# The first expert's first 384 rows multiplied in the tail of the attention, with the last 512 destinations routed behind them

## The chip, the cores and the metric

The kernel runs on one core of one Trainium2 chip. The metric is the device time of one execution in microseconds (us); the median of 7 executions is compared. A profile is one further execution under the hardware profiler. Its engines are PE (matrix products; PEld is its weight load), DVE (vector), ACT (activation functions), POOL (GpSimd) and SP (which only starts DMAs); each runs its own instructions strictly in order.

## The reference

The model has 3125 nodes of 256 features and 103125 directed edges, and four residual blocks:

```python
x = x + gat3(layernorm(x), src, dst)          # three graph-attention layers
x = x + moe_top2(layernorm(x))                # 16 experts, two per node
x = x + relu(n @ W + segment_sum((n @ M)[src], dst)),  n = layernorm(x)
x = x + moe_top1(layernorm(x))                # 8 experts, one per node
```

An attention layer gives each destination the softmax-weighted sum of its sources' rows. In the second block a node's logits are `n @ gate_w + gate_b`; its two largest, as a softmax over those two, weigh the outputs of two experts, each `(silu(n @ w1[e]) * (n @ w2[e])) @ w3[e]` with a hidden width of 512. The change lies where the first block ends and the second begins.

## The kernel before, in words

**The third attention layer** (L1371 to L1534, `i == 2`, called `last`). The 3125 destinations are cut into 13 groups (`GROUPS`, L1133): twelve of 256, which are two tiles of 128 partitions, and one of 53. For a group, the loop over `s` goes through 25 tiles of sources. DVE makes the weights `pm` of 128 sources by 256 destinations (L1448), and PE multiplies them into `acc` in PSUM (L1451), once for each of the two destination tiles; every such product is recorded as two PE instructions. Six `pm` buffers (pool `dp`) let DVE run ahead. The short group packs six source tiles into one `few` (L1439, L1441), and PE multiplies it at L1443. `acc` has two buffers, so that one group can be divided while the next is multiplied.

What follows a group is put in the list `later` (L1503 to L1506) with the step `s` of the next group at which it is written into the program: `divide` (L1476) at 8, `norm` at 9, `gate` at 11, `send` at 14, all some steps earlier for the group before the short one (`sooner`, L1502). The framework's scheduler then orders each engine's instructions, by priorities and its own model, and sets all waits; only inside `tc.manual_schedule()` (before: the second layer alone, L1403) does the order written by hand stand.

**The router** (`Router.group`, L608). `norm` takes mean and variance of each row (L619, L620), the square root on ACT (L621), loads ACT's table for the exponential ahead (`table`, L552 and L622), and writes the attention's output to `sums` in DRAM (L624), to which the experts' outputs are added later. `gate` normalises a row (L632), transposes it on PE (L637), copies it (L639), multiplies it by `gate_w` (L641) and adds the bias (L642). `send` finds the two largest logits with two runs of `first_max` (L241 to L249), makes the two weights (L650 to L656), counts the rank of each node among those sent to its expert by two small products (L664, L665) with a running sum `pre` (L662), turns it into a row number in `rows0` (L667 to L673), and sends the node's row, with its number and weight behind it, to that place for both experts by indirect DMAs of POOL (L680). `rows0` holds NP = 3200 rows for each expert; the expert takes the first 384 (`EACH` = 3 tiles), and what goes beyond is handled in "more" slots of 64 rows. `finish` (L686) makes the table of these slots, after 32 products (L693) of which nothing is read but which keep PE running.

**The experts** (`routed_experts`, L727). `turn(e)` loads 384 rows (L748) and transposes them (L753, L754); `fetch(e)` loads the expert's three weights of 512 KB; `first` multiplies by `w1` and `w2` (L778) with SiLU (L781) and product (L782); `second` multiplies by `w3` (L793), weighs (L796) and adds into `sums` by an indirect DMA of POOL that accumulates (L798). After the experts 3, 5, 7, 9 and 11 a pair of "more" slots runs (`first_more`, L805), with weights in `room`; if there are more than ten slots, the branch at L880 runs the others. At the end `sums` is read back (L886). All 16 experts go through this loop.

**Buffers.** The pool `big` has two large buffers. During the third layer one holds that layer's sources and the other the layer's output `y_out` (L1379); then `room` takes the sources' buffer.

## Time and profile before

| what | us |
| --- | --- |
| median of 7 runs (lowest, highest) | 1880.77 (1872.89, 1882.78) |
| the profiled execution, its own time | 1868.43 |
| its span, first to last instruction | 1866.7 |
| PE busy in the span | 1775.3 (95%) |
| DVE / ACT / POOL busy | 1016.2 / 722.1 / 491.3 |
| last product of the third layer ends (L1443) | at 1059.32 |
| first product of expert 0 starts (L778) | at 1083.07 |
| first product of expert 1 starts (L778) | at 1099.49 |

All places in time are microseconds from the start of the span. A row of the timeline gives start, duration, engine, line, operation, output and inputs with their shape, the number of instructions merged into the row (x4), and in brackets how long the engine stood idle before it and what ended that. A row of the table by stretches gives the stretch, its length, the busy time of each engine with its instructions, TensorE's granted clock as a share of full speed, the busy share of the DMA engines and GB/s. The chain of waits follows the work that ended last backwards, in order of time.

### The profile page before, as it was taken

The numbers are of one execution on the slowest core, as the hardware profiler recorded it, in microseconds if no ns is written. First come the engines' busy times: TensorE is split into PE (matmuls) and PEld (weight loads), VectorE is DVE, ScalarE is ACT, GpSimd is POOL, SyncE is SP. The second block draws the span as 40 slices with busy tenths as digits, with TensorE's granted clock in tenths as the row PEclk, the third lists the DMA queues.
The fourth block names the chain that finished last, engine by engine and source line by source line (L and its number), as shares of the span: only waits on it lengthen the run. The fifth ranks groups of instructions, "written<-read, shape, count | busy, mean of one in ns | idle before, by whom it ended". The sixth has DMA issues, their size and how long they took to land. (4 is left out here: it accounts for less than half of the span.)

```text
span 1866.7 us, 27222 instructions
## 1 busy us (share of the span) xinstructions
PE 1775.3 (95%) x9225; PEld 1383.8 (74%) x9225; DVE 1016.2 (54%) x2875; ACT 722.1 (39%) x2072; POOL 491.3 (26%) x634
## 2 busy tenths in 40 slices
PE   6999999999798999999999799999989999999997
PEld 4788888887577887788888666666668887455786
DVE  6888888875466777677777622222244222333221
ACT  3766767671011111122222211121127999455221
POOL 4210110000566775032322322333310000122121
PEclk9999999999899999999999899999999999999999
DMA  4111223757333332121111285877430000723894
GB/s 116 33 46 48 66 63 136 316 225 298 78 83 85 87 87 77 30 66 40 49 44 43 73 248 156 239 199 191 110 89 1 1 1 1 237 117 153 258 301 125
DMA packets 123698, 215.43 MB, mean 115 GB/s; under 512 B 14795, under 2 KB 86641, under 8 KB 123512
## 3 DMA queue, kind: packets, MB, share of 16 engines
q1 hardware_dynamic: 83700, 134.23, 21.5%
q0 software_dynamic: 24704, 56.84, 11.7%
q10 hardware_dynamic: 15138, 22.44, 3.8%
q8 instruction: 79, 1.29, 0.3%
q14 instruction: 77, 0.63, 0.1%
HBM read 122.54 MB, written 92.61 MB: 115 GB/s over the span
## 5 line engine op out<-in xcount | busy, mean ns | idle before, releaser
L1451 PE MATMUL acc<-big,pm 128*128 128x257 f32 x3400 | 796.8, 386 | 22.2 <-issue 15.6
L1451 PEld LDWEIGHTS acc<-big,pm 128*128 128x128 f32 x3400 | 633.4, 192 | 116.8 <-issue 20.1
L1448 DVE SCALAR_TENSOR_TENSOR pm<-tau,big,counts 128x256 f32<-128x256 f32 x850 | 398.6, 487 | 139.3 <-PE acc L1451 113.0
L1994 POOL DMA_INDIRECT apart_row<-apart_rows,apart_who x172 | 179.7, 1045 | 94.1 <-issue 44.2
L778 PE MATMUL ps_h<-xsT,w 128*128 128x384 f32 x512 | 168.4, 487 | 0.6 <-ACT xsT L754 0.6
L1603 PE MATMUL acc<-msg,cr 128*128 128x512 f32 (+1 forms) x625 | 157.9, 403 | 0.1
L778 PEld LDWEIGHTS ps_h<-xsT,w 128*128 128x128 f32 x512 | 96.8, 190 | 66.9 <-issue 1.9
L1603 PEld LDWEIGHTS acc<-msg,cr 128*128 128x128 f32 (+1 forms) x625 | 114.7, 185 | 29.2 <-ACT cr L1599 1.2
L1599 ACT ACTIVATE cr<-counts 128x256 fp32r<-128x256 uint8 (+1 forms) x325 | 130.5, 402 | 14.1 <-PE acc L1603 7.0
L1860 ACT CAST counts<-acc_c 128x500 uint8<-128x500 f32 (+1 forms) x155 | 96.0, 678 | 94.5 <-PE acc_c L1850 94.2
L1835 DVE TENSOR_TENSOR ohk<-iota_k,key 128x2016 f16<-128x2016 f16 (+1 forms) x79 | 94.4, 1195 | 20.4 <-PE acc_c L1850 20.2
L781 ACT ACTIVATE silu<-ps_h 128x384 f32<-128x384 f32 x64 | 31.4, 490 | 182.2 <-PE ps_h L778 180.1
L798 POOL DMA_INDIRECT sums<-y,who x48 | 74.7, 1556 | 92.7 <-DVE y L796 71.0
L782 DVE TENSOR_TENSOR hid<-silu,ps_h 128x384 f32<-128x384 f32 x64 | 35.4, 554 | 112.6 <-PE ps_h L778 107.7
L1829 ACT ACTIVATE ohs<-iota_s,low 128x128 f16<-128x128 f16 x286 | 94.1, 401 | 0.0
L936 PE MATMUL ps_H<-big,t_w 128*128 128x512 f32 (+1 forms) x224 | 93.1, 552 | 0.8 <-ACT H L938 0.5
L1351 ACT ACTIVATE yT<-ps_m 128x256 f32<-128x256 f32 (+1 forms) x25 | 9.5, 379 | 204.0 <-PE ps_m L1349 173.8
L1064 PE MATMUL ps_y<-t_wd,hsT 128*128 x384 | 87.1, 379 | 0.3 <-ACT hsT L1112 0.3
L793 PE MATMUL ps_o<-w,hid 128*128 128x256 f32 x384 | 87.2, 379 | 0.0
L1850 PEld LDWEIGHTS <-ohs 128*128 128x128 f16 x1250 | 77.7, 98 | 10.9
L1850 PE MATMUL acc_c<-ohk,ohs 128*128 128x125 f16 x1250 | 84.5, 218 | 0.0
L1221 PE MATMUL ps_m<-we,yT 128*128 128x258 f32 (+1 forms) x248 | 71.7, 409 | 11.5 <-ACT yT L1351 6.1
(398 smaller groups left out, 2159.6 us busy)
## 6 DMA issues: line engine op xcount, KB each, us to landing
rows<-empty SPq DMA_DIRECT2D x16, 2564.0 KB
w<-in_L_ffn_w_dram ACTq DMA_DIRECT2D x42, 512.0 KB
big<-in_L_ffn_w_dram SPq DMA_DIRECT2D x30, 512.0 KB
hs<-rows SPq DMA_DIRECT2D x23, 641.0 KB
rows<-empty SPq DMA_DIRECT2D x16, 516.0 KB
t_wd<-in_L_ffn_Wd_dram SPq DMA_DIRECT2D x8, 1024.0 KB
big<-in_L_ffn_Wd_dram SPq DMA_DIRECT2D x6, 1024.0 KB
xs<-rows SPq DMA_DIRECT2D x15, 387.0 KB
```

The source lines that it names most:

```text
L778: nc.tensor.matmul(ps, w[:, k, j * P:(j + 1) * P], xsT[:, k], start=(k == 0), stop=(k == KD - 1))
L793: nc.tensor.matmul(ps, hid[:, j, q * P:(q + 1) * P], o[:, j], start=(j == 0), stop=(j == nh - 1))
L936: nc.tensor.matmul(ps[:, :n], a[:, k, j * P:(j + 1) * P], xnT[:, k, c:c + n], start=(k == 0), stop=(k == KD - 1))
L1448: nc.vector.scalar_tensor_tensor(pm[:, :n], tau[:, :n], now.rho[:, of:of + 1], edges[:, of, :n], op0=OP.max, op1=OP.mult)
L1451: nc.tensor.matmul(acc[:r, j, :D + 1], pm[:, q:q + r], now.h[:, of, :D + 1], start=(s == 0), stop=(s == NT - 1))
L1599: nc.scalar.activation(cr[:, :n], edges[:, s, :n], AF.Copy, accum_out=seen[:, a * NT + s:a * NT + s + 1])
L1603: nc.tensor.matmul(acc[:r, j].rearrange("p h d -> p (h d)"), cr[:, q:q + r], msg[:, s].rearrange("p h d -> p (h d)"), start=(s == 0), stop ...
L1829: nc.scalar.activation(far[:, i], self.iota_s, AF.Abs, scale=-1.0, bias=self.low32[:, batch, i:i + 1])
L1835: nc.vector.tensor_tensor(to[:, i:tiles].rearrange("p t (x u) -> p t x u", u=2), iota.rearrange("p (x u) -> p x u", u=2)[:, None].to_broad ...
L1850: nc.tensor.matmul(acc[:, u], ohs[:, i], ohk[:, i, :KEYS], start=(t == 0), stop=(t == TW - 1))
L1860: nc.scalar.copy(to[:, :, d0 % PAIR:d0 % PAIR + whole * WIN].rearrange("p s (u d) -> p u s d", u=whole), acc[:, :whole])
L1994: nc.gpsimd.indirect_dma_start(out=row[:, j], out_offset=None, in_=self.table[:, :], in_offset=bass.IndirectOffsetOnAxis(ap=self.who[:, q ...
```

## The change: what it does

1. **Order of the third layer's parts** (`LAST_PARTS`): groups 0 to 9, then the short group, then group 10 (tiles 20, 21), then group 11 cut into two parts of one tile (22, 23). The group before the short one is divided beside it, but normalised, gated and sent one part later, beside group 10 (`more = NT`). Tile 23's routing comes after all attention products.
2. **Expert 0's rows are settled early.** After the short group is sent, `reserve` raises the first free place of expert 0 to 384 if fewer nodes have come so far, so that the last 512 destinations (tiles 20 to 23) lie behind its first 384 rows. `expert.load` then loads these rows on SP, behind the scatters of all tiles sent so far; `expert.turn` transposes them at step 16 of the last part. Expert 0's weights are loaded at the layer's start into the buffer that was `y_out`'s; `y_out` becomes a small tile for each part.
3. **The tail is written by hand** (`tc.manual_schedule()`): tile 23's routing stands first on each engine, and expert 0's products, SiLUs and second products lie between its steps. `first(acc, j, u)` is a quarter of `w1` (u = 0) or `w2` (u = 1): four PE instructions. `finish` comes in three pieces between them; its 32 idle products go.
4. **The expert loop starts at 1.** Expert 1's weights, rows and transposed rows lie in `room`, its weights are fetched by SP as soon as the layer's sources are free. Expert 0's outputs are scattered after that (`expert.send`), and expert 1's scatters wait for them. Experts 2 and 3 are fetched by SP behind expert 1's transposed rows.
5. The last block's hidden weights (`hidden_weights`) are asked for in the third part of the layer rather than after it.

The diff, cut to its core:

```diff
+def behind_all(tc, made, others):
+
+    for other in others:
+        tc.add_manual_dep(made.ins, other.name, mybir.DependencyInfo(mybir.DependencyClass.Sync, mybir.DependencyReason.DATA),
+                          reason="rows of different tokens")
+    return made
...
+    def reserve(self, pp):
+
+        nc = self.nc
+        ps = pp.tile([P, 1], F32, name="ps_z")
+        nc.tensor.matmul(ps, self.every, self.pre[:, self.sent, 0:1], start=True, stop=True)
+        nc.vector.tensor_scalar(self.bump, ps, -1.0, float(EACH * P), op0=OP.mult, op1=OP.add)
+        nc.vector.tensor_scalar(self.bump, self.bump, 0.0, None, op0=OP.max)
+        nc.vector.tensor_tensor(self.first[:, 0:1], self.first[:, 0:1], self.bump, op=OP.add)
...
+        def again(i, t):
+            other = rp.tile([P, ROW0], F32, name="row2")
+            nc.scalar.copy(other[:, :D], own[i][:, :D])
+            for row in (own[i], other):
+                nc.gpsimd.tensor_copy(row[:, D:D + 1], self.node[:, t:t + 1])
+            others.append(other)
...
-            table(nc, wp, rstd[:, 1], AF.Exp)
+            table(nc, wp, rstd[:, 1], AF.Silu if apart else AF.Exp)
...
+                if between:
+                    between()
...
-            if t0 + n == NT - 1:
+            if before_last:
                 table(nc, wp, m2, AF.Sqrt)
-            nc.vector.tensor_scalar(wt[:, 0], m2, 1.0, None, op0=OP.add)
-            nc.vector.reciprocal(wt[:, 0], wt[:, 0])
-            nc.vector.tensor_tensor(wt[:, 1], m2, wt[:, 0], op=OP.mult)
+
+            def weigh():
+                nc.vector.tensor_scalar(wt[:, 0], m2, 1.0, None, op0=OP.add)
+                nc.vector.reciprocal(wt[:, 0], wt[:, 0])
+                nc.vector.tensor_tensor(wt[:, 1], m2, wt[:, 0], op=OP.mult)
+            if not apart:
+                weigh()
             sel = wp.tile([P, n, NX0], BF16, name="g_sel")
...
+            if apart:
+                weigh()
...
+                if not apart:
+                    again(i, t)
+                for j, row in enumerate((own[i], others[i])):
...
-        nc.scalar.copy(self.pre[0:1, 0], total)
-        keep_warm(nc, pp.tile([P, (NT + 1) * NX0], F32, name="ps_x"), self.every, self.pre.rearrange("p t e -> p (t e)"), 32)
+        places = cp.tile([1, NX0], F32, name="more_total")
+        nc.vector.tensor_copy(places, total)
+        nc.vector.tensor_tensor(places[:, 0:1], places[:, 0:1], self.bump[0:1], op=OP.add)
+        total = places
+        yield
...
+        yield
...
+    def load(self, scatters):
+        behind_all(self.tc, self.nc.sync.dma_start(self.xs, self.rows[:EACH * P].rearrange("(q p) f -> p q f", p=P)),
+                   scatters)
+
+    def turn(self, pp):
+        nc = self.nc
+        for q in range(EACH):
+            ps = pp.tile([P, KD, P], F32, name="ps_m")
+            for k in range(KD):
+                nc.tensor.transpose(ps[:, k], self.xs[:, q, k * P:(k + 1) * P], self.ident)
+            nc.scalar.copy(self.xsT[:, :, q * P:(q + 1) * P], ps)
+        nc.gpsimd.tensor_copy(self.who, self.xs[:, :, D])
+
+    def first(self, ap_, j, u):
+        nc = self.nc
+        if u == 0:
+            self.ps[j] = ap_.tile([P, 2, CHUNK], F32, name="acc")
+        for k in range(KD):
+            nc.tensor.matmul(self.ps[j][:, u, :EACH * P], (self.a, self.b)[u][:, k, j * P:(j + 1) * P], self.xsT[:, k],
+                             start=(k == 0), stop=(k == KD - 1))
+
+    def glu(self, j):
+        nc, ps = self.nc, self.ps.pop(j)
+        nc.scalar.activation(self.hid[:, j], ps[:, 0, :EACH * P], AF.Silu)
+        nc.vector.tensor_tensor(self.hid[:, j], self.hid[:, j], ps[:, 1, :EACH * P], op=OP.mult)
+
+    def second(self, pp, q):
+        nc, nh = self.nc, HID0 // P
+        ps = pp.tile([P, D], F32, name="ps_m")
+        for j in range(nh):
+            nc.tensor.matmul(ps, self.hid[:, j, q * P:(q + 1) * P], self.o[:, j], start=(j == 0), stop=(j == nh - 1))
+        nc.vector.tensor_scalar(self.xs[:, q, :D], ps, self.xs[:, q, D + 1:D + 2], None, op0=OP.mult)
+
+    def send(self):
+        self.scatters = [
+            independent(self.tc, "sums0", self.nc.gpsimd.indirect_dma_start(
+                out=self.sums[:, :], out_offset=bass.IndirectOffsetOnAxis(ap=self.who[:, q:q + 1], axis=0),
+                in_=self.xs[:, q, :D], in_offset=None, bounds_check=NP + CAP0 - 1, oob_is_err=True, compute_op=OP.add))
+            for q in range(EACH)]
+
...
         def turn(e):
-            xs = xp.tile([P, nq, ROW0], F32, name="xs")
-            for q, n in ((0, nq),) if e else ((0, 1), (1, 1), (2, nq - 2)):
+            xs = xs_1 if e == 1 else xp.tile([P, nq, ROW0], F32, name="xs")
+            for q, n in ((0, nq),) if e > 1 else ((0, 1), (1, 1), (2, nq - 2)):
                 at = e * NP + q * P
-                nc.sync.dma_start(xs[:, q:q + n], rows[at:at + n * P].rearrange("(q p) f -> p q f", p=P))
-            xsT = xp.tile([P, KD, EACH * P], F32, name="xsT")
+                dma = nc.sync.dma_start(xs[:, q:q + n], rows[at:at + n * P].rearrange("(q p) f -> p q f", p=P))
+                if e == 1:
+                    behind_all(tc, dma, expert.rows_sent)
+            xsT = xsT_1 if e == 1 else xp.tile([P, KD, EACH * P], F32, name="xsT")
...
+            a, b, o = weights_1 if e == 1 else [pool.tile([P, k, f], F32, name=name) for pool, k, f, name in (
+                (ep, KD, HID0, "w1"), (ep, KD, HID0, "w2"), (op_, nh, D, "w3"))]
+            if 1 < e < 4:
 
                 for to in (a, b, o):
                     nc.gpsimd.tensor_copy(to[:, 0, 0:1], behind)
-            dma = (nc.sync if 0 < e < 3 else nc.scalar).dma_start
+            dma = (nc.sync if e < 4 else nc.scalar).dma_start
             dma(a, w1[e].rearrange("(k p) h -> p k h", p=P))
             dma(b, w2[e].rearrange("(k p) h -> p k h", p=P))
...
+                independent(tc, f"sums{e}", made)
+                if e == 1:
+                    behind_all(tc, made, expert.scatters)
...
-        turned = turn(0)
+        weights = fetch(1, None)
+        turned = turn(1)
+        expert.send()
+        x = block(big)
         behind = turned[1][:, 0, 0:1]
-        for e in range(NX0):
-            a, b, o = fetch(e, behind)
-            if e == 2:
+        for e in range(1, NX0):
+            a, b, o = weights if e == 1 else fetch(e, behind)
+            if e == 3:
                 load(behind)
             xs, xsT = turned
             hid, s = first(xsT, a, b)
...
+PARTS_OF = [(a, c, n) for a, (c, n) in enumerate(GROUPS)]
+LATE = 3
+LAST_PARTS = PARTS_OF[:10] + PARTS_OF[12:] + PARTS_OF[10:11] + [(11, 11 * PAIR + q, P) for q in (0, P)]
...
-                    y_out = block(big)
-                    nc.gpsimd.memset(y_out[:, NT - 1], 0.0)
+                    expert = make_first(block(big, ROW).rearrange("p t d -> p (t d)"))
...
-                for a, (c, n) in enumerate(GROUPS):
-                    if apart_now and a < APART:
-                        continue
+                parts = LAST_PARTS if last else PARTS_OF[APART:] if apart_now else PARTS_OF
+                for here, (a, c, n) in enumerate(parts):
                     tiles = [(q, (c + q) // P, min(P, n - q)) for q in range(0, n, P)]
+                    following = parts[here + 1:here + 2]
+                    short = bool(following) and following[0][2] <= P // 2
 
                     edges = counts_of(counts, a)
+                    if c > GROUPS[a][0]:
+                        edges = edges[:, :, c - GROUPS[a][0]:]
...
+                        if last and (a, s) == (2, 0):
+                            during(expert.a[:, 0, 0:1])
...
+                    if last:
+                        y_out = wl.tile([P, KD, D + 2], F32, name="we")[:, :, :D]
+                        if n <= P // 2:
+                            nc.gpsimd.memset(y_out[:, 0], 0.0)
...
-                    sooner = 2 if a == len(GROUPS) - 2 else 5 if i == 0 and a == len(GROUPS) - 1 else 0
-                    later.append((8 - sooner, divide))
-                    if last:
-                        norm, gate, send = router.group(wp, rp, zp, y_out, tiles[0][1], len(tiles))
-                        later += [(9 - sooner, norm), (11 - sooner, gate), (14 - sooner, send)]
+                    sooner = 2 if short else 5 if i == 0 and a == len(GROUPS) - 1 else 0
+                    if last and following:
+                        norm, gate, choose, send, again = router.group(wp, rp, zp, y_out, tiles[0][1], len(tiles),
+                                                                before_last=len(parts) - here == 2)
+                        more = NT if short else 0
+                        if len(parts) - here == 2:
+                            sooner = 4
+                        later += [(8 - sooner, divide), (9 - sooner + more, norm), (11 - sooner + more, gate),
+                                  (14 - sooner + more, choose), (14 - sooner + more, send)]
+                        if len(parts) - here == LATE + 1:
+                            later += [(14, lambda: router.reserve(zp)), (14, lambda: expert.load(router.scatters))]
+                        if len(parts) - here == 2:
+                            later.append((16, lambda: expert.turn(pp)))
+                    elif last:
+                        norm, gate, choose, send, again = router.group(wp, rp, zp, y_out, tiles[0][1], len(tiles), apart=True)
...
-            router.finish(wp, zp, over)
+            def between():
+                expert.first(ap_, 1, 0)
+                expert.glu(0)
+                again()
+                table(nc, wp, expert.hid[:, 0, 0:1], AF.Exp)
+
+            with tc.manual_schedule():
+                divide()
+                expert.first(ap_, 0, 0)
+                expert.first(ap_, 0, 1)
+                norm()
+                gate(between)
+                expert.first(ap_, 1, 1)
+                expert.first(ap_, 2, 0)
+                expert.first(ap_, 2, 1)
+                choose()
+                send()
+                finish = router.finish(wp, zp, over)
+                next(finish)
+                expert.glu(1)
+                expert.first(ap_, 3, 0)
+                expert.first(ap_, 3, 1)
+                expert.glu(2)
+                next(finish)
+                expert.glu(3)
+                for _ in finish:
+                    pass
+                for q in range(EACH):
+                    expert.second(pp, q)
...
+        def during(behind):
+            hidden.extend(hidden_weights(nc, early, *(i["L1_ffn_" + n] for n in ("W1", "b1", "Wg", "bg")), behind))
```

## The prediction

> **What bounds the kernel now.** I read the table of busy time by stretches first, then PE's timeline in the stretch that is not full, then the chain of waits. PE is busy for 95% of the span, so only a stretch where it lacks work can give time. By stretches, over the end of the third attention layer and the start of the experts:
>
> ```profile
> 1032.60:1052.20 19.60, 19.60 (x98) 16.63 (x96) 13.19 (x51) 4.96 (x10) 4.96 (x11) 1.00 0.04 14
> 1052.20:1059.40 7.20, 7.04 (x56) 3.56 (x55) 5.10 (x18) 2.80 (x7) 2.91 (x7) 1.00 0.26 91
> 1059.40:1083.10 23.70, 12.78 (x61) 7.06 (x61) 14.32 (x83) 5.82 (x15) 7.03 (x14) 0.71 0.36 113
> 1083.10:1099.50 16.40, 16.40 (x63) 11.49 (x64) 3.19 (x6) 4.40 (x8) 2.96 (x11) 1.00 1.00 342
> ```
>
> PE is full before 1059.40 and after 1083.10. Between them it counts 12.78 us, and PE's timeline shows what this is:
>
> ```profile
> 1060.60 0.62 PE L641 MATMUL ps_z<-gate_w,g_xT 128*128 128x16 f32 x4 [0.37 <-ACT g_xT L639]
> 1064.94 0.21 PE L664 MATMUL ps_z<-g_sel,before 128*128 128x32 bf16 x1 [3.73 <-DVE g_sel L660]
> 1065.14 0.19 PE L665 MATMUL ps_z<-pre,every 128*128 128x32 bf16 x1
> 1066.93 0.69 PE L637 MATMUL ps_x<-ident,row 128*128 128x128 f32 x2 [1.61 <-DVE row L632]
> 1068.08 1.04 PE L641 MATMUL ps_z<-gate_w,g_xT 128*128 128x16 f32 x4 [0.46 <-ACT g_xT L639]
> 1072.25 0.20 PE L664 MATMUL ps_z<-g_sel,before 128*128 128x16 bf16 x1 [3.13 <-DVE fm_hot L249]
> ...
> 1073.17 7.94 PE L561 MATMUL ps_x<-pre,every 128*128 128x416 bf16 x32 [0.25 <-ACT pre L692]
> 1081.64 0.85 PE L753 MATMUL ps_x<-ident,xs 128*128 128x128 f32 x6 [0.53 <-DMA xs<-rows]
> ```
>
> 7.94 of the 12.78 are products nobody reads; the rest serves the routing of the last tiles, which DVE, ACT, POOL and DMA carry. So some 24 us pass from the last attention product (1059.32) to expert 0 (1083.07), and then the chain is all PE:
>
> ```profile
> 1083.07 10.59 PE ps_h L778 x32
> 1093.65 0.66 PE ps_x L753 x6
> 1094.31 5.18 PE ps_o L793 x24
> 1099.49 5.80 PE ps_h L778 x18
> ```
>
> Expert 1 starts at 1099.49, that is 40.2 us after the last attention product. I call that product's end T0 and count from it; the change is worth what it takes from these 40.2 us, less what it adds ahead of T0.
>
> **From T0 to expert 1, routing.** One tile is routed after T0 instead of three. Divide: last time 1052.28 (end of products) to 1053.3 with one tile, mean and variance from T0+1.1. Row ready 1.6 later, by the single tile's rows: 0.46 (from 1062.57 to 1063.03), 0.20, the root 0.29 and the way to and from ACT, reciprocal 0.2, row 0.45: 2.7. Transposes 0.44: 3.15. The copy waits on ACT for the new SiLU table, loaded ahead behind the root (1.28 plus 0.20): 3.5, done 3.9. PE meanwhile makes 4 instructions of the expert (32 take 10.32, so 1.29): 4.45; gate 0.5: 4.95. From the bias at 1069.16 to the sum at 1072.40 DVE took 3.2: 8.15. The rank stands on PE behind 12 more expert instructions (3.87): 8.8, so 9.2. Rank to place numbers 1072.52 to 1073.56, and a hop: 10.3. From there to the second scatter's issue 1073.56 to 1076.55: 13.3. Landing: the rows were asked for at 1078.71, but the chain names DVE's last table entry (L724, ends 1078.52) for it, so 2.16 is an upper bound: 15.4. Rows asked for to first product 1078.71 to 1083.07, 4.36: expert 1 could start at **T0+19.8**.
>
> **From T0 to expert 1, expert 0's own work.** Last `first` quarters: `acc` has two buffers, so j = 3 waits for `glu(1)`, which DVE does after the place numbers: 10.3, two small operations 0.35, product 0.55: 11.2. Two quarters: 13.8. `second`: 3 x 1.73. Here a new wait is late: `ps_m` has two buffers, and the third `second` needs DVE's weighing of the first, which stands behind `glu(3)` (0.65) and the long piece of `finish` (1074.79 to 1078.52: 3.75): 18.2, weighed 18.7. The third product ends at 20.4, and expert 1's transposes and copy (1081.64 to 1083.07: 1.43) put its first product at **T0+21.8**. This is later than the routing, so I take it: 21.8 against 40.2 is **-18.4**. The idle products' 7.94 lay beside DVE, POOL and the DMA, and are worth nothing by themselves.
>
> **The clock.** Granted 0.71 in the stretch after 1059.40: after 3.73 us of idle PE, two transposes took 0.69 where 0.41 is usual. My sum leaves gaps of under 2 us. If one grew to that size, expert 1 would start slow: the idle products came back from 0.62 within some 4.4 us, so at most 2.2.
>
> A rule that speaks against the change: the tail needs the tables Sqrt, SiLU, Exp, SiLU. The trace has the load at 1.28, and the next activation 0.02 later:
>
> ```profile
> 1066.01 1.28 ACT L555 ACT_TABLE_LOAD   x1
> 1067.31 0.20 ACT L555 ACTIVATE table<-g_rstd 128x1 f32<-128x1 f32 x1
> ```
>
> The Trainium skill, "ScalarE: Activation LUTs", What ACT_TABLE_LOAD costs, gives the load about 1.28 us too, but adds a drain of 1.38 us to every switch. With two loads ahead of what PE waits for (before the copy, before `glu(1)`) that would be an estimate of 2.8 us off the gain. The rows above show no such drain, so the sum stands without it.
>
> **Ahead of T0.** The same attention products are made. Added on PE: in the old order 18 to 23 were routed before T0 but for the gate of 22 and 23; now 18 to 22 and 24 are. That is two single routings (0.38 + 0.51 + 0.4 each, from L637, L641, L664, L665) less 0.44: about +2.0. Expert 0's transposes, 0.85, and `reserve`, 0.2. Together +3.0, since PE is full there. The terms (L1337) stay the same in sum.
>
> DVE is the open point. A pair of tiles has a period of 23.8 us (L637 at 1014.43 and 1038.26) with DVE busy 17.8 in such a period, 25 x 0.48 of it for `pm`. A one-tile part halves PE's products (10.8) but not DVE's fixed cost. The trace has no `pm` of 128 x 128; neighbours are 0.48 (128 x 256) and 0.21 (`few`, 128 x 53). I take 0.30, between them by width. Part 22: 7.5 and the pair's routing 5.8 make 13.3 against PE's 12.9. Part 23: 7.5 and a single routing 5.2, 12.7 against 12.6. The part of group 10, with two routings beside it: 23.5 against 25. So DVE and PE are level, and six `pm` buffers now cover 6 x 0.43 instead of 6 x 0.87. I take 1.5 us of stalls. With 0.21 there are none; with 0.48 the two parts would lack some 9.
>
> T0 moves by 3.0 + 1.5 = **+4.5**.
>
> **Costs taken at nothing.** `expert.load` blocks SP until the scatters of 21 tiles have landed; the rows of `x` for tiles 22 and 23 and the `sums` stores queue behind it. Those scatters end some 3 us into part 22 (group 10's 25 us cover choice, places and six issues of 1.28), the rows come 5 us later, the transposes stand 13 us later still. Expert 0's 1.5 MB at the layer's start and the hidden weights (now asked for at 792.7, used at 1591) meet DMA at 0.12 to 0.14 busy. Expert 1's weights are asked for at T0 and have 21 us. Expert 1's scatters wait on POOL for expert 0's; an accumulation took 9.01 (1371.35), so about 2 us of waiting, with only other scatters and index casts behind. The first slots' 3 MB must wait until expert 1 has left `room` (T0+38) and are needed 28 us later; at 342 GB/s (1083.10 to 1099.50) they take 9.
>
> **Sum.** -18.4 + 4.5 = -13.9 from expert 1 on, where everything follows as before. The profiled execution took 1868.43, so 1854.5. It lies below all seven timed runs; against their median, 1880.77 - 13.9 = **1867**.
>
> **Rivals.**
> (a) *The gain is partly given back*, -7, 1874. Either DVE's `pm` is nearer 0.48 (+7), or expert 2's weights are late: SP takes them only behind POOL copies (L764), which may queue behind expert 0's three scatters (1.61 + 0.30 each, so 5 us after expert 1's start); 1.5 MB at 342 GB/s take 4.6, in time for 15.5; with the slots' 3 MB ahead of them, 5.5 late. For it: SP did issue a slot's load (1082.44) ahead of weights (1083.29). Against: the new slot loads can't start then.
> (b) *Slower: the routing chains lie open in the one-tile parts.* Place: parts 22 and 23. DVE waits in order for ACT's root and table, PE's gate and rank, with `pm` behind. One open chain is what now passes from 1059.36 to 1073.56, 14.2; six buffers cover 2.6; two open parts cost 23.2, giving -18.4 + 3.0 + 23.2 = +8, 1889. It decides from 15 us of stalls on. Against it: in the pair periods the same chain leaves PE 0.24 idle.
> (c) *It doesn't do what it says.* If more than ten slots were needed, L880's branch would run eleven pairs, each at least 9 us of loads: about +100, 1980. Counted from the reference's inputs, expert 0 gets 394 nodes outside the last 512, so `reserve` adds nothing, and the slots stay at exactly ten. Under 0.01.
> (d) *More*: T0+19.8 holds and DVE doesn't stall, -20.4 + 3.0 = -17.4, 1863.
>
> **How the numbers follow.** 0.2% is 3.8 us, about what a measurement of this kernel can tell from no change. Forecast and (d) 0.60, (a) 0.24, all faster: 0.84. Same 0.06 (stalls between (a) and (b)). Slower 0.10, nearly all (b). Range 1859 to 1877: (d) with a median that itself moves by some 4 (the seven lie within 10), up to where (a) ends.
>
> **What would show it.** Right: first products of L778 for expert 1 near 1086, PE full from T0 but for gaps of 1 to 2 us before j = 3 and the third `second`; no L561 at the tail; parts 22 and 23 of some 13 us each. Wrong: DVE without a gap in those parts and PE waiting for `pm`; the third `second` late for another reason than DVE's weighing of the first; PE idle inside expert 1 for weights.

## The result and the profile after

The changed kernel takes **1865.63 us** (median of 14 runs) against 1880.77 us (35 runs): a ratio of 0.9916 with the interval 0.9898 to 0.9934, so 12 to 19 us faster. The forecast was 1867, within 1859 to 1877.

The profiled execution took 1862.84 us (span 1861.0). That is only 5.6 less than the profiled execution before, and here a whole span misleads. The third layer's first product comes at 766.88 in the one and at 773.77 in the other, although the change touches little ahead of it. Over all profiled executions that point lies between 722 and 782 us, and the runs on one of the chips, where the kernel before takes 1827 us instead of 1880, have it at 722 to 736 throughout. So I compare stretches inside an execution, from points that every variant has: L3, the third layer's first product; T0, the last attention product's end; E1 and E2, the first products of expert 1 and expert 2, each by its own start in PE's timeline. For the kernel before that is 1099.33:

```profile
1099.33 10.48 PE L778 MATMUL ps_h<-xsT,w 128*128 128x384 f32 x32
```

The 1099.49 of the table of times before and of the prediction is the place of that product in the chain of waits, which gives it to PE only when the product before it has ended. So the prediction's 40.2 is 40.0 here, and 0.2 of the difference in the second row below is only this.

| us | before | after | change | forecast |
|---|---|---|---|---|
| L3 to T0 | 292.44 | 295.45 | +3.0 | +4.5 |
| T0 to E1 | 40.0 | 24.85 | -15.2 | -18.4 |
| E1 to the end | 767.38 | 766.97 | -0.4 | 0 |
| L3 to the end | 1099.83 | 1087.27 | -12.6 | -13.9 |

E2 to the end, which no edit touches, takes 749.4 to 752.8 us over all profiles, so -0.4 behind E1 can't be told from nothing.

These are the stretches of the profile after, with the columns of the first fence of the prediction: the busy time of PE, weight loads, DVE, ACT, POOL, each with its instructions, then the granted clock, the DMA share and GB/s.

```profile
1018.30:1043.60 25.30, 25.26 (x129) 21.72 (x129) 19.65 (x93) 7.83 (x17) 7.46 (x14) 1.00 0.10 33
1043.60:1056.60 13.00, 12.54 (x62) 9.91 (x61) 11.42 (x45) 3.41 (x8) 3.01 (x7) 1.00 0.24 70
1056.60:1069.00 12.40, 12.40 (x66) 10.33 (x65) 11.62 (x72) 6.76 (x13) 5.37 (x12) 1.00 0.15 53
1069.00:1094.10 25.10, 20.58 (x79) 13.30 (x78) 14.81 (x65) 7.92 (x15) 8.45 (x13) 0.93 0.48 147
```

The rows are the part of group 10, the two one-tile parts 22 and 23, and the tail from T0 (1069.22) to E1 (1094.07). The parts have the forecast lengths (25, about 13 and 13) and PE is full in them but for half a microsecond. Before, PE was busy for 12.78 of the 23.7 us up to expert 0's first product, 7.94 of them for products that nobody reads, and expert 0 then took 16.4 more; now it is busy for 20.58 of the 25.1 us up to expert 1's, and all of that is read by somebody. What PE does there, by its timeline of the profile after (the bracket is the idle time before the first instruction of a row, and who ended it):

```profile
1069.05 2.75 PE L811 MATMUL acc<-big 128*128 128x384 f32 x8
...
1073.83 4.13 PE L811 MATMUL acc<-big 128*128 128x384 f32 x12
1077.79 0.17 PE L706 MATMUL ps_z<-g_sel,before 128*128 128x16 bf16 x1
...
1080.10 4.42 PE L811 MATMUL acc<-big 128*128 128x384 f32 x8 [1.65 <-DVE big L817]
1084.32 3.81 PE L823 MATMUL ps_m<-big 128*128 128x256 f32 x16
1087.96 0.82 PE L867 MATMUL ps_x<-ident,big 128*128 128x128 f32 x6
1089.83 1.99 PE L823 MATMUL ps_m<-big 128*128 128x256 f32 x8 [1.05 <-DVE big L824]
...
1093.37 0.30 PE L867 MATMUL ps_x<-ident,xs 128*128 128x128 f32 x1 [1.43 <-DMA xs<-rows]
```

L811 is `first`, L823 `second`, L867 the transposes of a routed expert's rows (`big` holds expert 1's, `xs` expert 2's). Two of the three waits were foreseen, j = 3 for `glu(1)` and the third `second` for DVE. The third wait and one duration were not. Eight instructions of `first` take 2.75 at 1069.05 and **4.42** at 1080.10. And the wait of 1.43 is for the rows of **expert 2**, whose transposes stand ahead of expert 1's first product. The chain of waits of the profile after says why those rows are late:

```profile
1089.18 0.20 DVE more L771
1089.38 0.02 issue
1089.40 0.02 SPq L860
...
1089.51 3.30 DMA xs<-rows
1092.81 0.56 issue
1093.37 0.30 PE ps_x L867
```

SP asks for them (L860) only when DVE has written the last entry of the slot table (L771): the theory is that the rows' buffer lies where `finish` had its temporary tiles, and tables_apart below tests it.

### The profile page after: what moved, and what is told of

Its sections match the earlier page's. It is cut to its first block, busy times and chain, and to the rows that moved or that the text cites. A ratio compares the mean times of both kernels' runs of the same rounds, so it can differ in the third digit from the quotient of the medians.

```text
span 1861.0 us, 27219 instructions
## 1 busy us (share of the span) xinstructions
PE 1769.3 (95%) x9196; PEld 1380.6 (74%) x9196; DVE 1019.9 (55%) x2933; ACT 727.2 (39%) x2080; POOL 490.6 (26%) x634
## 5 line engine op out<-in xcount | busy, mean ns | idle before, releaser
L1577 PE MATMUL acc<-big,pm 128*128 128x257 f32 x3400 | 797.8, 386 | 20.3 <-issue 12.7
L1574 DVE SCALAR_TENSOR_TENSOR pm<-tau,big,counts 128x256 f32<-128x256 f32 (+1 forms) x875 | 401.5, 478 | 123.8 <-PE acc L1577 104.7
L891 PE MATMUL ps_h<-xsT,w 128*128 128x384 f32 x448 | 147.3, 487 | 0.0
L891 PEld LDWEIGHTS ps_h<-xsT,w 128*128 128x128 f32 x448 | 84.7, 190 | 58.0 <-issue 1.9
L911 POOL DMA_INDIRECT sums<-y,who x45 | 70.0, 1556 | 75.8 <-DVE y L909 63.7
L2194 DVE SCALAR_TENSOR_TENSOR apart_acc<-apart_row,apart_co,apart_acc 128x257 f32<-128x257 f32 x167 | 80.8, 484 | 1.6
```

Of the source, the lines that this page charges most:

```text
L891: nc.tensor.matmul(ps, w[:, k, j * P:(j + 1) * P], xsT[:, k], start=(k == 0), stop=(k == KD - 1))
L1574: nc.vector.scalar_tensor_tensor(pm[:, :n], tau[:, :n], now.rho[:, of:of + 1], edges[:, of, :n], op0=OP.max, op1=OP.mult)
L1577: nc.tensor.matmul(acc[:r, j, :D + 1], pm[:, q:q + r], now.h[:, of, :D + 1], start=(s == 0), stop=(s == NT - 1))
```

## The experiments

The theory: the tail gained in two ways, by expert 0's products lying beside the routing and by one tile instead of three being routed after T0; the 3 us or so that are missing there are mostly PE's lower clock behind the gap at 1078.4 and the wait for expert 2's rows. Its rivals: that the routing alone gives the gain and the interleaving little; that DVE's order in the tail (`finish` ahead of the weighing) is what is lost; and, ahead of T0, that the one-tile parts have hardly any cover left and a little more would make them stall.

All variants are of the changed kernel unless said otherwise. The points of each profiled execution (those from routing_then_expert to three_buffers ran on a chip where the kernel before takes 1827, the last four on one where it takes 1879):

| us | L3 to T0 | T0 to E1 | T0 to E2 | last 8 of `first` |
|---|---|---|---|---|
| before | 292.44 | 40.0 | 56.2 | |
| after | 295.45 | 24.85 | 40.6 | 4.42 |
| routing_then_expert | 293.94 | 31.04 | 47.3 | (32 in 12.42) |
| gap_filled | 293.95 | 23.39 | 39.2 | 2.85 |
| weighed_first | 293.94 | 21.10 | 38.4 | 2.85 |
| whole_group | 293.34 | 27.78 | 43.6 | 4.52 |
| tables_apart | 293.96 | 24.16 | 39.8 | 4.53 |
| all_three | 293.95 | 21.36 | 36.9 | 2.85 |
| before_without_idle_products | 292.22 | 42.52 | 58.7 | |
| three_buffers | 299.57 | 24.91 | 40.7 | 4.47 |
| changed_again | 295.11 | 24.93 | 40.7 | 4.54 |
| weighed_and_filled | 295.34 | 21.10 | 37.4 | 2.85 |
| changed_look | 294.89 | 25.00 | 40.8 | 4.54 |
| weighed_look | 294.89 | 22.79 | 40.1 | 4.54 |

**Expert 0's products behind the routing** instead of beside it:

```diff
                 divide()
-                expert.first(ap_, 0, 0)
-                expert.first(ap_, 0, 1)
                 norm()
                 gate(between)
-                expert.first(ap_, 1, 1)
-                expert.first(ap_, 2, 0)
-                expert.first(ap_, 2, 1)
                 choose()
                 send()
                 finish = router.finish(wp, zp, over)
                 next(finish)
-                expert.glu(1)
-                expert.first(ap_, 3, 0)
-                expert.first(ap_, 3, 1)
-                expert.glu(2)
+                for j in range(4):
+                    expert.first(ap_, j, 0)
+                    expert.first(ap_, j, 1)
+                    expert.glu(j)
                 next(finish)
-                expert.glu(3)
```

(`between` loses its `first` and `glu` too.)

> As the changed kernel, but in the tail tile 23's whole routing is written first and all of expert 0's products after it, instead of between its steps. S is the stretch from the third layer's first product to expert 1's first product: 332.6 before, 320.3 in the changed kernel's profile. My theory (expert 0's products fill PE's waits inside the routing): the 24 instructions that now lie beside the routing (7.7 us) move behind the place numbers, partly at a low clock because PE stands idle first, so S grows by 5 to 6, to about 326, and the gain falls from 15 to about 9 us. Rival (the gain comes from routing one tile instead of three after the last product, and from expert 0's rows being there early; the interleaving is worth nothing, since scatter, landing and load leave room enough): S stays within 1 of 320.

T0 to E1 grows to 31.04, by 6.2; the time is 1815.96 against 1827.63 (ratio 0.9933, 0.9916 to 0.9950). That ratio lies between the changed kernel's two (0.9916 and 0.9939), which were measured on the other chip, and the changed kernel itself was not run on this one; so the 6.2 rests on the stretch, not on the time. The stretch is good for it: where the tail's program is the changed kernel's, T0 to E1 is 24.85 to 25.00 in four profiles on both chips. PE's timeline of this variant shows the routing's waits open again, the clock lost with them, and DVE's `finish` late for the third `second`:

```profile
1024.06 0.69 PE L664 MATMUL ps_x<-ident,row 128*128 128x128 f32 x2 [2.68 <-DVE row L659]
...
1029.22 0.19 PE L706 MATMUL ps_z<-g_sel,before 128*128 128x16 bf16 x1 [2.97 <-DVE g_sel L695]
...
1030.06 12.42 PE L811 MATMUL acc<-big 128*128 128x384 f32 x32
...
1049.22 1.99 PE L823 MATMUL ps_m<-big 128*128 128x256 f32 x8 [2.49 <-DVE big L824]
```

So of the 15.2 us of the tail the interleaving holds 6.2. The other 9.0 (40.0 less 31.04) remain without it: one tile instead of three after T0, and 384 rows that wait for no routing. No run tells these two apart. The 32 products in a row took 12.42 against 10.3 at full clock, so part of the 6.2, some 2 us, is clock: busy time that overlaps keeps it up.

**The gap filled** with 8 products that nobody reads:

```diff
                 next(finish)
+                keep_warm(nc, zp.tile([P, (NT + 1) * NX0], F32, name="ps_x"), router.every,
+                          router.pre.rearrange("p t e -> p (t e)"), 8)
                 expert.glu(1)
```

> As the changed kernel, with 8 products that nobody reads (about 1.4 us) in PE's gap before expert 0's last quarters. My theory: in that gap of some 2 us the clock was lost, and the 8 instructions behind it took 4.42 instead of 2.75; with the gap filled they take 2.75, and since the chain to expert 1 runs through them, S falls by 1.7 to 318.6. Rival (the clock fell for what lay before, or falls on any such tail): the 8 instructions stay at about 4.4 and S at 320.3.

PE's timeline of this variant:

```profile
1028.77 1.58 PE L561 MATMUL ps_x<-pre,every 128*128 128x416 bf16 x8
1030.48 2.85 PE L811 MATMUL acc<-big 128*128 128x384 f32 x8
```

The eight instructions take 2.85 instead of 4.42 and E1 is 1.46 earlier. Products without a reader are worth 1.5 us here, for the clock alone.

**DVE weighs first**, the long piece of `finish` follows:

```diff
                 expert.glu(3)
-                for _ in finish:
-                    pass
                 for q in range(EACH):
                     expert.second(pp, q)
+                for _ in finish:
+                    pass
```

> As the changed kernel, but the long piece of finish is written behind expert 0's second products and their weighing. My theory: DVE's long piece holds up both the third second product (1.05 us idle) and, through it, the rows of expert 2, whose transposes stand on PE ahead of expert 1; with the piece behind, expert 1 starts 22.1 after the last attention product instead of 24.8, S falls by 2.7 to 317.6, and expert 2's rows come later but in time. Rival (expert 1 waits for its own rows, that is for scatter and landing): S stays at 320.3; rival of the other sign (expert 2's rows, now 3 us later, hold PE ahead of expert 1): S grows by 3 to 323.

> The weighing ahead of the long piece of finish, a further look: in the first look the gap was there (1.64) and the 8 instructions behind it took 2.85. If that comes from the edit, they take 2.85 again; if from the execution, 4.4 may come here.

PE's timeline of weighed_first:

```profile
1029.59 2.85 PE L811 MATMUL acc<-big 128*128 128x384 f32 x8 [1.64 <-DVE big L817]
1032.28 5.49 PE L823 MATMUL ps_m<-big 128*128 128x256 f32 x24
...
1039.84 10.59 PE L891 MATMUL ps_h<-big 128*128 128x384 f32 x32 [0.54 <-issue]
1051.23 0.85 PE L867 MATMUL ps_x<-ident,xs 128*128 128x128 f32 x6 [0.81 <-DMA xs<-rows]
```

The three `second` run through (24 in 5.49) and E1 is 3.75 earlier, more than expected, because here the eight instructions kept their clock with the same gap in front of them (1.64). A second profile of the same kernel, weighed_look, has the same gap, 4.54 for the eight, and E1 2.1 earlier: that is the order alone. Part of it is given back: the slot table is now finished after E1, so the rows of expert 2 come later and PE waits for them inside expert 1 (0.81 and 0.87). At E2 some 0.6 us is left in weighed_look.

**Both tiles of the last group routed after T0**, part 11 whole again:

```diff
-LATE = 3
-LAST_PARTS = PARTS_OF[:10] + PARTS_OF[12:] + PARTS_OF[10:11] + [(11, 11 * PAIR + q, P) for q in (0, P)]
+LATE = 2
+LAST_PARTS = PARTS_OF[:10] + PARTS_OF[12:] + PARTS_OF[10:12]
```

(`between` then runs after the second tile, and copies the rows of both.)

> As the changed kernel, but group 11 stays whole, so that tiles 22 and 23 are both routed after the last product. My theory: ahead of the last product one single routing less and no one-tile parts, so it comes 1.5 to 2 earlier; in the tail a second tile's statistics, row, transposes, gate and two more scatters add 2.5 to 3.5 on the chain; S grows by 1 to 321. Rival (the split costs more on DVE than it saves): S falls below 319.

T0 is 0.6 earlier than in the variants run beside it (293.34 against 293.94), less than expected, and T0 to E1 is 2.9 longer than in the changed kernel. Against its neighbours that is 2.3 slower in sum. (S is 321.1, as expected, but by luck: without this edit it is 318.8 on this chip, put together from the other variants, not 320.3.) The split into two parts is worth it, though its parts have less cover.

**The slot table's tiles apart** from the rows' buffer: `finish` gets its temporaries in free columns of expert 0's buffer.

```diff
-                finish = router.finish(wp, zp, over)
+                finish = router.finish(Spare(expert), zp, over)
```

(The class `Spare`, which hands out these columns, is left out.)

> As the changed kernel, but the small tiles of finish lie in free columns of expert 0's buffer instead of the pool whose memory the rows of expert 2 take over. My theory: the load of expert 2's rows waits for DVE's last table entry only because it is given that memory; without this it is asked for several us earlier, its transposes no longer hold PE, and expert 1 starts about 1 earlier (the third second product still waits for the weighing): S about 319.3. Rival (that wait is the DMA's, or lies beside the weighing anyway): the load is asked for as late as before and S stays at 320.3.

SP now asks for expert 2's rows ahead of DVE's last table entry, at T0+16.1 instead of T0+20.3, so the shared memory was what held them:

```profile
1042.07 0.91 SPq L882 DMA_DIRECT2D xs<-rows  x2
1046.07 0.18 DVE L771 TENSOR_TENSOR more<-big 1x32 int32<-1x32 f32 x1
```

E1 is 0.7 earlier (24.16). The wait of 1.43 becomes several of 0.24 to 0.33, for the rows and for ACT's copies of expert 2's transposes, so this step's own worth is half of the wait that the trace showed. The clock was lost here too (4.53 for the eight, behind a gap of 1.65).

**All three edits**, and the **first two** (weighed first and the gap filled):

> As the changed kernel, with the gap filled, the weighing ahead of the long piece of finish, and finish's tiles apart, all three together. My theory: the three waits are one after the other on the same chain, so S falls by 1.7 and 2.7 and little more, to about 316, where the routing's own chain (scatter, landing, load: expert 1 at 19 to 20 after the last product) is next; the time falls by about 4 against the changed kernel, to 1861 to 1862. Rival (one wait replaces another): S stays within 1 of 320, and the time at 1865.

> As the changed kernel, with the weighing ahead of the long piece of finish and the gap filled, but finish's tiles where they were. My theory: expert 1 starts 21 after the last attention product as with the weighing alone, never at a low clock, and expert 2's rows hold PE inside expert 1 for about 0.8; the time is 2 to 4 below the changed kernel. Rival (the rows of expert 2, asked for later, or the filling, take it back): no difference in the time, within 1 of the changed kernel.

The costs don't add up. All three give 21.36 to E1, no less than weighed_first alone; with the rows early, two of expert 2's transposes stand ahead of expert 1 again and wait 0.62. Seen from E2 the order is as it should be: 40.6 to 40.8 in the changed kernel, then 37.4 with two edits, 36.9 with three. The times: all_three 1809.99 against 1827.35 (ratio 0.9904, 0.9887 to 0.9921). weighed_and_filled 1862.83, ratio 0.9913 (0.9881 to 0.9945), where the changed kernel run beside it has 0.9939 (0.9918 to 0.9960). The traces say 3.3 us better at E2; the intervals overlap, so the times don't settle it.

**The kernel before without its idle products** (32 of them to 1):

> The kernel before with 1 instead of 32 products that nobody reads in its tail. My theory (they are worth nothing by themselves, but hold the clock): expert 0's first 32 instructions take about 2 longer than 10.6, and S grows from 332.6 to about 334.5. Rival (they delay the tail, and part of the gain is their removal): S falls.

T0 to E1 is 42.52, 2.5 longer. PE's timeline of this variant:

```profile
1028.35 0.51 PE L561 MATMUL ps_x<-pre,every 128*128 128x416 bf16 x1 [0.25 <-ACT pre L692]
1037.29 1.51 PE L753 MATMUL ps_x<-ident,xs 128*128 128x128 f32 x6 [8.43 <-DMA xs<-rows]
```

After 8.43 idle the six transposes take 1.51 instead of 0.85. The idle products lay beside the routing, as the prediction said, but held the clock for what followed. A change that takes such products away must leave PE busy in their place, and this one nearly does.

**Three `pm` buffers instead of six:**

```diff
-        with tc.tile_pool(name="dp", bufs=6) as pmp, tc.tile_pool(name="ds", bufs=2) as sp, \
+        with tc.tile_pool(name="dp", bufs=3) as pmp, tc.tile_pool(name="ds", bufs=2) as sp, \
```

> As the changed kernel, with 3 instead of 6 buffers for the weights pm. It tests the rival that the routing chains lie open in the one-tile parts: six buffers cover 2.6 us there, three 1.3. If cover is what holds them, the stretch from the short group's first product to the last attention product (57.8) grows by 3 to 6, mostly in the one-tile parts, while the pair parts before it (23.8 each) grow by under 1; if DVE's total work is what matters, both stay within 1.

L3 to T0 grows by 5.6 against the variants with six on the same chip, and the pair parts ahead of the short group keep their 237.65 us. Most of it lies in part 22, where PE is busy for 11.46 of 14.00, at a clock of 0.88. That is what the expectation said, but not for its reason. PE's timeline of this variant in and behind part 22:

```profile
1007.00:1021.00 14.00, 11.46 (x52) 9.57 (x52) 8.47 (x31) 5.07 (x10) 1.46 (x6) 0.88 0.20 60
```

```profile
1011.96 0.44 PE L802 MATMUL ps_m<-ident,big 128*128 128x128 f32 x2 [2.54 <-DMA big<-rows]
...
1025.35 0.70 PE L1577 MATMUL acc<-big,pm 128*128 128x257 f32 x2 [0.43 <-DVE pm L1574]
```

With three buffers the scheduler put two of expert 0's six transposes (L802) into part 22, ahead of attention products; in the changed kernel all six stand in part 23. There PE waited 2.54 us for expert 0's rows, and lost the clock for it: 0.88 over 14.00 us is another 1.7. Together that is 4.2 of the 5.6. The waits for `pm` are 0.43, no more than with six (0.45 in the profile after). So this run doesn't show the mechanism of rival (b), and hardly tests it; it shows that expert 0's transposes, too early in PE's order, hold up the attention.

**The changed kernel again**, twice, unchanged:

> The changed kernel itself once more, beside the next ones. My theory: S, from the third layer's first product to expert 1's first product, is 12 shorter than the kernel before's 332.5, wherever the start of the third layer falls, and the time 10 to 16 shorter. The stretch from the short group to the last attention product is either 57.8 as in the first profile (then 56.3 in the other runs is due to their edits) or 56.3 (then it belongs to the execution). The low clock behind PE's gap (8 instructions in 4.4 instead of 2.8) may be there or not: if it comes and goes with the same gap, it is the execution's, not the program's.

> The changed kernel, a further look at the same question: is the clock low behind PE's gap of 1.6 to 2.1 before expert 0's last quarters in every execution? If the low clock belongs to the program, the 8 instructions take 4.4 again; if to the execution, 2.8 in some.

T0 to E1 is 24.93 and 25.00, and the eight instructions take 4.54 both times: tail and clock loss repeat to 0.15 us. S is 320.0 and 319.9, 12.4 and 12.6 shorter than before. The stretch from the short group to T0 is 57.5 and 57.2: it goes with the chip (57.2 to 57.8 in the five profiles on this one, 56.3 in those on the other whose edits lie behind T0), not with the edits. The time of changed_again is 1868.10 against 1879.27 (ratio 0.9939, 0.9918 to 0.9960).

## Why the prediction was right, point by point

**The routing path.** Right to within 0.8 us, each step a little early: place numbers at T0+10.1 (forecast 10.3), the second scatter's issue ended at T0+12.9 (13.3), the rows asked for at T0+14.6 (15.4).

**Expert 0's own work is later than the routing.** Right, and for the reason given: the third `second` waits for DVE's weighing behind `finish`. Putting the weighing first took 2.1 away, as that step implies. But E1 came at T0+24.85 and not T0+21.8, and this is where the sum was off, by two terms. The clock was given at most 2.2 us "if one grew", and taken at zero in the sum; it cost 1.5 to 1.7, because a gap of some 2 us was enough. And expert 2's transposes had no term at all: I followed the rows of expert 1 and not what PE does next in its order. Their wait of 1.43 is not all loss, since the 1.43 that the sum gave to expert 1's transposes fell away: PE made them (1087.96) while it waited for the third `second`. From the end of that `second` (1091.82) to E1 2.25 us passed, 0.8 more than the 1.43, and tables_apart recovered 0.7. In the sum's terms, 4.42 for the two quarters' 2.6 and 2.25 for 1.43 make 2.6 of the 3.05 us.

**The idle products at nothing.** Right as a sum of PE's time; for the clock they were worth 2.5 us in the kernel before, which my sum set aside.

**Ahead of T0.** +2.4 to +3.0 where the kernel before takes about 1880, and about +1.7 where it takes 1827 (293.95 less 292.22, the latter from the variant without idle products); forecast +4.5. The term that was mis-sized is the stalls. These are the rows of the whole stretch, before and after:

```profile
766.88:1059.32 292.44, 289.97 (x1438) 247.64 (x1437) 216.65 (x745) 62.02 (x124) 84.08 (x164) 1.00 0.16 49
773.77:1069.22 295.45, 292.84 (x1458) 248.91 (x1458) 224.16 (x829) 69.05 (x139) 87.63 (x171) 1.00 0.17 54
```

PE's own share, forecast at 3.0, is 2.9 here (2.8 and 2.5 in the repeats, 2.1 on the other chip). PE was idle for 2.47 us before and is for 2.61 now (2.35 and 2.42 in the repeats): no stalls were added, where I had 1.5. DVE's rows for `pm` and PE's for the products that wait for it, from the profile after:

```profile
1047.68 1.90 DVE L1574 SCALAR_TENSOR_TENSOR pm<-tau,big,counts 128x128 f32<-128x128 f32 x7
```

```profile
1046.09 1.35 PE L1577 MATMUL acc<-big,pm 128*128 128x257 f32 x4 [0.17 <-DVE pm L1574]
1047.73 2.44 PE L1577 MATMUL acc<-big,pm 128*128 128x257 f32 x10 [0.28 <-DVE pm L1574]
```

Seven `pm` take 1.90 in a row, 0.27 each, a little under the 0.30 that I took between 0.21 and 0.48. The two chips differ by 0.9 to 1.5 us in this stretch; why is open.

**The table loads.** The row, not the rule, was right to use: the load for `glu(1)` takes 1.28 (from 1076.80) and the next activation starts at 1078.09. No drain shows.

**The rivals.** (a) No wait for expert 2's weights: E1 to E2 takes 15.8 us, before 16.2. Part of the gain was given back, by 3.2 in the tail, but neither of the two mechanisms that I named did it. (b) Not seen: PE's waits for `pm` stay below 0.5 us, with six buffers and with three. (c) The slots are as before (their pairs make the same 160 products in both profiles). (d) Fell, for the clock and expert 2's rows.

Together -12.6 from L3 to the end against -13.9, and -15.1 in the medians (-11.2 for changed_again). The term that was too good for the change (+3.2 in the tail) and the one that was too bad (-1.5 ahead of T0) partly cancel, and the median moves by some microseconds with the earlier layers: that the median met the forecast to 1.4 us is partly luck.

## What to carry to other kernels

In a tail that one serial chain sets, do both: route less after the last product, and lay work that needs no result of the chain on the idle engine; here the first, together with expert 0's rows settled early, was worth some 9 us and the second 6. When such a sum is made, follow the instructions of the bounding engine in their own order up to the product that is meant, and ask for each what it waits for, also when it serves a later step; and ask whose memory its buffer was. Compare stretches between points that both kernels have, when an untouched part of the program moves by more than the change.

## What the runs showed of the hardware

**A gap of about 2 us can cost the clock, and it matters where it falls.** In these traces the granted clock is either full or at 0.50, and each low stretch lasts one or more steps of 3.41 us (but for the last of an execution, which its end cuts off). The low stretches of one execution lie on one grid of such steps: in the profile after, 1081.23, where one begins, is 107 steps of 3.4133 behind 716.00, where another does. These are rows cut to that grid around the gap (PE's busy time is the first figure behind the length, its granted clock the third column from the right), first of the profile after, then of weighed_first, whose low step from 714.22 to 717.63 sets the grid:

```profile
1077.82:1081.23 3.41, 1.46 (x8) 0.88 (x7) 2.89 (x18) 1.13 (x3) 1.32 (x3) 1.00 0.04 16
1081.23:1084.64 3.41, 3.41 (x7) 1.90 (x6) 0.63 (x4) 0.08 (x1) 1.27 (x3) 0.50 0.19 69
1084.64:1088.05 3.41, 3.41 (x17) 2.82 (x17) 2.86 (x6) 0.41 (x1) 0.00 (x0) 1.00 0.41 121
```

```profile
1024.83:1028.25 3.42, 2.84 (x12) 1.50 (x10) 2.52 (x17) 2.13 (x4) 0.18 (x1) 1.00 0.47 162
1028.25:1031.66 3.41, 2.07 (x7) 1.27 (x8) 2.93 (x19) 0.23 (x1) 2.25 (x4) 1.00 0.11 39
1031.66:1035.07 3.41, 3.41 (x16) 2.61 (x15) 1.04 (x2) 0.49 (x1) 0.34 (x2) 1.00 0.31 92
```

From 1077.99 to 1080.10 PE did one product of 0.17 and was idle for the rest. That gap lies in one step of the grid, and the next step is at half; 3.41 us at half are the 1.7 us that the products lost. In weighed_first the grid cuts the same gap in two, and the clock stays full. The clock was lost in seven of the eight executions with this gap unfilled (1.64 to 1.71 behind the last small product), and in each of the seven PE was busy for 1.4 to 1.6 us of the step that held the gap; it was kept in one, weighed_first; in three with the gap filled it was kept each time. Since only one execution kept it, how much of a step must be idle is not known. The Trainium skill, "TensorE: Matmul & The Clock Gate", Part 1: The HAM clock gate, says that the clock is halved after an idle window of about 3.4 us, and that the window runs freely. The halving, the length of the step and the free run agree; but here a step of which PE was busy for 1.4 to 1.6 us was enough, so the measurement decides: a gap of 2 us isn't safe.

**The second layer's time.** L3 lies at 767 to 782 us where the kernel before takes about 1880, and at 722 to 736 where it takes 1827; the first layer's last products end at 453 to 465 on both, so the difference arises between there and L3. From L3 to the end the one variant that was profiled on both (weighed_first and weighed_look) takes 1083.9 and 1087.5, and 1.7 of these 3.6 us are the clock in the tail. What makes the second layer longer isn't settled here.
